# Second-layer softmax denominators by 32x32 transposes and row sums, with a moved sum written in place, narrower low products and an earlier range check

## The chip, the cores and the metric

The kernel runs on one core of a Trainium2 chip. The metric is the device time of one execution in microseconds (us). The core's engines are TensorE (PE for its matmuls, PEld for its weight loads), VectorE (DVE), ScalarE (ACT), GpSimd (POOL) and SyncE (SP, which issues DMAs). Each works through its own queue in order, and semaphores tie them together.

## The reference, cut to what matters

Two attention layers follow each other on four images of 64 x 64 tokens with 256 channels, in fp32:

```python
# layer 0: N = 4096 tokens, C = 256, q and k of 32 channels, v of 256
q, k, v = x @ Wq + bq, x @ Wk + bk, x @ Wv + bv
attn = softmax(q @ k.T)                 # per image, 4096 x 4096
x = gamma * (attn @ v) + x
# layer 1: f and g of 32 channels, v of 128, Wo from 128 to 256
f, g, v = x @ Wf + bf, x @ Wg + bg, x @ Wh + bh
beta = softmax(g @ f.T)
x = x + (beta @ v) @ Wo + bo
```

## The kernel before, in words

The kernel never subtracts a maximum: it takes exp of the raw scores, divides at the end by the sum of the exponentials, and at its very end checks that all denominators, values and gamma lay in a safe range (a general path, not taken with these inputs, stands behind that check).

**Blocks and steps.** The work is one long list of `Step`s: for each image `b`, each layer `l`, each block `j` of queries, each step `i` over the keys. The first layer has 16 blocks of 256 queries and 8 steps of 512 keys; the second has 8 blocks of 512 queries and 16 steps of 256 keys. So there are 512 steps of the first layer and 512 of the second, in 32 blocks, one execution long. Each step handles a tile of 128 x 1024 scores: `scores` (L532 the products, L542 and L544 the exponentials), products with the values (`products_first`, L580, and `products_second`, L598), and on VectorE what follows.

**Split and whole steps.** In every step of the first layer and in the steps `SPLIT1` of the second, the exponentials are cut into parts of reduced precision: `high` (L542, ACT), `low` = p - high (`cut_low`, L555, DVE) and `d` (`cut_both`, L560, DVE). Such products run as one instruction each. In the other steps the whole fp32 `p` is multiplied (two instructions for each product).

**Denominators.** In the first layer the values carry two more columns (`W` = 258 instead of `C` = 256): column 256 holds 1.0 in the high part, 0.0 in the low part and -EPS in the d part, so the denominators come out of the products themselves. The second layer's accumulator is turned the other way (128 channels x 512 queries), so there the sums over the keys are made apart: DVE adds up the `p` tiles of a block (`add_up`, L571 and L573) into `p_sum`; the tiles of the steps `MOVED_SUMS` are left to DMAs that POOL issues, the first as a copy (L548) and the others accumulating (L550), into the buffer `p_sum_moved`. `end_second` (run when a block's last step is traced) adds the accumulator's second half to the first (L655), adds `p_sum_moved` to `p_sum` (L657) and the two halves of `p_sum` to each other (L658, `sums`, 128 x 512). Each of the 128 partitions then still holds its own part of the sum, and queries lie along the row. For each of the four groups of 128 queries, `output(t)` multiplies the attention output by `Wo` (L665), multiplies `sums` with a column of ones (L666), which adds over the partitions and turns the result, takes the reciprocal (L668), scales (L671, `y`) and adds `y` to the output in DRAM by an accumulating DMA (L673).

**What sets the order.** `plan` puts units of work into the steps of a block: the four `output` units of the block before into steps 1 to 4, and the projections (L392 transpose, L422, L464 and what follows) of the next image into steps of this one. The loop at L733 calls, in each step: `cut_both`, `cut_low` of the next step, `add_up`, `scores` two steps ahead, the units, the products. The framework places all semaphores and gives out the buffers; an instruction whose buffer is not free yet is queued later than its place in the program says, and a POOL DMA may be queued earlier when its buffer is free. For example the loads of queries (L493, `q`, four DMAs) of block j + 2 stand in POOL's queue near the end of block j.

**Buffers.** `wide` gives tiles of 128 x 1024: tag "t" has two buffers (`high`, and `p` of split steps of the second layer), "p" three, "l" two (`low`, and `d` of the second layer), "d" one (`d` of the first layer, `p_sum`), "e" one (`p_sum_moved`). Small tiles of 128 x 256 (`small`) have four. The accumulators (`acc`) have one buffer each. PSUM tiles for side products (`side_psum`) have two.

**End.** After the last block the range check runs (L805 to L820), writes a count (`off`), and every engine loads that count and branches past the general path.

Of the kernel before, what the change touches and what calls it, by code (L numbers as in the profile page):

```python
# [50 lines left out]
F32 = mybir.dt.float32  # L51
# [3 lines left out]
ALU = mybir.AluOpType  # L55
AX = mybir.AxisListType

P = 128
QB = 512
QB0 = 256  # L60
NT = QB // P
S = 32
# [3 lines left out]
AHEAD = 3  # L66

SPLIT1 = (0, 3, 5, 8, 11, 13)
MOVED_SUMS = (0, 4, 7, 9, 12)

# [166 lines left out]
def fast_path(ctx: ExitStack, tc: tile.TileContext, x, w0, w1, wo, bo, gamma, out, off):  # L239

    nc = tc.nc
    B, N, C = x.shape
# [24 lines left out]
    def wide(tag, name, dtype=F32):  # L267
        return work.tile([P, 2 * QB], dtype, tag=tag, bufs={"d": 1, "e": 1, "p": 3}.get(tag, 2), name=name)
# [39 lines left out]
    ones = const.tile([P, 1], F32, name="ones")  # L308
    nc.vector.memset(ones, 1.0)

    inverse = const.tile([P, 2, B * N // P], F32, name="inverse")
    seen_v = const.tile([P, 2, B * NH], F32, name="seen_v")
    down = const.tile([P, 1], F32, name="down")
# [32 lines left out]
    def side_psum(name):  # L346
        return ps_side.tile([P, QB], F32, tag="side", name=name)
# [25 lines left out]

    xT, x_parts, k_t, v_t, halves = {}, {}, {}, {}, {}
    qk_dram, x1_dram = {}, {}
    q_t, moved_sums, first_p, waiting = {}, {}, [], {}


    def transpose_unit(b, l, h):
# [130 lines left out]
    def small(name):  # L510
        return work.tile([P, C], F32, tag="small", bufs=4, name=name)


    class Step:
# [8 lines left out]
        def scores(self):  # L523
            b, l, j, i = self.b, self.l, self.j, self.i
            n = 2 * QB // G[l]
            q0 = j * n % QB
            index = j * NI[1] + i
            tag = "pair" if l == 1 and index > 0 and index % 2 == 0 else "st"
            st = ps_main.tile([P, G[l], n], F32, tag=tag, name=f"st_{self.key}")
            for g in range(G[l]):  # L530
                kt = G[l] * i + g
                nc.tensor.matmul(  # L532
                    st[:, g, :],
                    k_t[b, l, kt // NT][:, kt % NT * P : (kt % NT + 1) * P],
                    q_t[b, l, j * n // QB][:, q0 : q0 + n],
                    start=True,
                    stop=True,
                )
            s_flat = st.rearrange("p g n -> p (g n)")
            if self.split:  # L540
                self.high = wide("t", f"high_{self.key}", F32R)
                nc.scalar.activation(self.high, s_flat, AF.Exp, bias=down)  # L542
            self.p = wide("t" if self.split and l == 1 else "p", f"p_{self.key}")
            nc.scalar.activation(self.p, s_flat, AF.Exp)  # L544
            if l == 1 and i in MOVED_SUMS:
                if i == MOVED_SUMS[0]:
                    moved_sums[b, j] = wide("e", f"p_sum_moved_{b}_{j}")
                    nc.gpsimd.dma_start(moved_sums[b, j], self.p)  # L548
                else:
                    nc.gpsimd.dma_start(moved_sums[b, j], self.p, accum_op=ALU.add)  # L550

        def cut_low(self):
            if self.split:
# [7 lines left out]
                    self.d, self.low.bitcast(F32), -UP, self.high.bitcast(F32), ALU.mult, ALU.add  # L561
                )

        def add_up(self, p_sum):
            if self.l == 0 or self.i in MOVED_SUMS:
                return
            kept = [i for i in range(NI[1]) if i not in MOVED_SUMS]
            if self.i == kept[0]:
                first_p.append(self.p)
            elif self.i == kept[1]:  # L570
                nc.vector.tensor_add(p_sum, first_p.pop(0), self.p)  # L571
            else:
                nc.vector.tensor_add(p_sum, p_sum, self.p)  # L573

        def products_first(self, acc, s, what):
            p, v, which = {
                "h": (self.high, "h", 0), "l": (self.low, "l", 0), "d": (self.d, "d", 1)
            }[what]
            for g in range(G[0]):
                nc.tensor.matmul(  # L580
                    acc[2 * s + which][:, :W],
                    p[:, g * QB0 + s * P : g * QB0 + (s + 1) * P],
                    v0[self.i][v][:, g, :],
                    start=self.first and what != "l" and g == 0,
                    stop=self.last and what != "h" and g == G[0] - 1,
                )
# [62 lines left out]
            nc.scalar.activation(o[h][:, :QB0], acc[0][:, h * QB0 : (h + 1) * QB0], AF.Copy, scale=1.0 + EPS)  # L649
        return o  # L650

    def end_second(b, j, acc, p_sum, o):
        key = f"{b}_{j}"
        for h in range(QB // QB0):
            nc.vector.tensor_add(o[h][:, :QB0], o[h][:, :QB0], acc[1][:, h * QB0 : (h + 1) * QB0])  # L655
        sums = work.tile([P, QB], F32, tag="sums", bufs=1, name=f"sums_{key}")
        nc.vector.tensor_add(p_sum, p_sum, moved_sums[b, j])  # L657
        nc.vector.tensor_add(sums, p_sum[:, :QB], p_sum[:, QB:])  # L658

        def output(t):  # L660
            def issue():
                tok = slice(t * P, (t + 1) * P)
                ps = side_psum(f"pso_{key}_{t}")
                part = o[t // NS][:, t % NS * P : (t % NS + 1) * P]
                nc.tensor.matmul(ps[:, :C], part, wo_sb, start=True, stop=True)  # L665
                nc.tensor.matmul(ps[:, C : C + 1], sums[:, tok], ones[:, :1], start=True, stop=True)  # L666
                n = (b * N + j * QB) // P + t
                nc.vector.reciprocal(inverse[:, 1, n : n + 1], ps[:, C : C + 1])  # L668

                y = small(f"y_{key}_{t}")  # L670
                nc.scalar.activation(y, ps[:, :C], AF.Copy, scale=inverse[:, 1, n : n + 1])  # L671
                row = j * QB + t * P
                nc.gpsimd.dma_start(out[b, row : row + P, :], y, accum_op=ALU.add)  # L673

            return issue

        return [output(t) for t in range(NT)]

    def run(units):
        for u in units:  # L680
            u()


    x_res = {}
# [10 lines left out]
    beyond = Step(B, 1, 0, 0)  # L695
    beyond.scores, beyond.split = nothing, False
    keys = [(b, l, j) for b in range(B) for l in range(2) for j in range(NB)][NB:]
    acc, p_sum, units = None, None, {}

    def plan(b, l, j, ends):  # L700

        units = {}

        def put(i, *some):
            units.setdefault(i, []).extend(some)

        if l == 0:

            if j >= 2:
                t, qk, v = project_units(b, 1, j - 2)  # L710
                put(0, t), put(4, qk), put(5, v)
            for n, u in enumerate(ends):
                put(1 + n, u)
            return units
        if j == 0:
            for n, u in enumerate(ends):
                put(1 + n, u)
            for n, h in enumerate((NH - 2, NH - 1)):
                t, qk, v = project_units(b, 1, h)
                put(6 * n, t), put(6 * n + 2, qk), put(6 * n + 3, v)  # L720
        else:
            for n, u in enumerate(ends):
                put(1 + n, u)
        if b + 1 < B:
            for h in range(NH):
                i = 12 + 7 * h - j * NI[1]
                for n, u in zip((0, 2, 3), project_units(b + 1, 0, h)):
                    if 0 <= i + n < NI[1]:
                        put(i + n, u)
        return units  # L730

    ends = bias_units()
    for n, s in enumerate(steps):  # L733
        b, l, j = s.b, s.l, s.j
        if s.first:
            units = plan(b, l, j, ends)
            acc = [ps_main.tile([P, QB], F32, tag=f"acc{a}", name=f"acc{a}_{b}_{l}_{j}") for a in range(2)]
            if l == 0:
                pair = ps_main.tile([P, 2, QB], F32, tag="pair", name=f"acc_pair_{b}_{j}")
                acc += [pair[:, a, :] for a in range(2)]  # L740
            if l == 1:
                p_sum = wide("d", f"p_sum_{b}_{j}")
        if l == 0 and s.last:
            x_res[b, j] = []
            for t in range(NS):
# [18 lines left out]

        s.cut_both()
        after.cut_low()
        s.add_up(p_sum)
        todo = units.get(s.i, [])

        if l == 1:  # L770
# [26 lines left out]
        while keys and halves.get(keys[0]) == 2 and (keys[0][:2] == (b, l) or keys[0][2] < over):  # L797
            load_k(*keys.pop(0))
        if s.last:
            ends = end_first(b, j, acc) if l == 0 else end_second(b, j, acc, p_sum, o)  # L800
    run(ends)

    good = small("good").rearrange("p (l n) -> p l n", l=2)  # L805
    nc.vector.tensor_scalar(good, inverse, 1.0 / SUM_MAX, None, ALU.is_ge)
    nc.vector.tensor_scalar(inverse, inverse, 1.0 / SUM_MIN, None, ALU.is_le)
    nc.vector.tensor_mul(good, good, inverse)
    nc.vector.tensor_scalar(seen_v, seen_v, VALUE_MAX, None, ALU.is_le)
    size = const.tile([P, 1], F32, name="size")  # L810
    nc.vector.tensor_mul(size, gamma_sb, gamma_sb)
    nc.vector.tensor_scalar(size, size, GAMMA_MAX**2, None, ALU.is_le)
    low = const.tile([P, 1], F32, name="low")
    for seen, axes in ((good, AX.XY), (seen_v, AX.XY)):
        nc.vector.tensor_reduce(low, seen, axes, ALU.min)
        nc.vector.tensor_mul(size, size, low)
    nc.vector.tensor_scalar(low, size, 1.0, None, ALU.is_lt)
    count = ps_side.tile([1, 1], F32, tag="side", name="count")
    nc.tensor.matmul(count, ones, low, start=True, stop=True)
# [51 lines left out]
```

## Time and profile before

| what | value |
|---|---|
| median of 3 runs | 3157.75 us (3157.27 to 3158.47) |
| the profiled execution's own time | 3156.87 us |
| its span, first to last instruction | 3155.1 us |
| granted TensorE clock, mean | 0.998 |
| a late block of the second layer (last image, nothing of a next image beside it) | 35.51 us |
| a block of the second layer with projections of the next image | 39.4 to 41.9 us |
| a block of the first layer, most | 28.2 to 28.5 us |

The profile is of one execution. Its page gives the busy time of each engine, the span in 40 slices, the DMA queues, the chain that ended last (followed back from the last instruction, at each step to what released it), the costliest groups of instructions and the DMA issues. A group line reads: line of the kernel, engine, operation, output <- inputs, partitions x elements, count | busy us in total, mean ns of one | idle time of the engine just before them and what ended it. Timelines give start us, duration us, engine, line, operation, with the idle time before it in brackets. Matmuls are pipelined: the duration of one overlaps the next, so what a matmul costs is read from one start to the next, or from the chain, whose pieces follow each other.

### The profile page before, as it was taken

What the parts mean: (1) busy time and instruction counts of PE and PEld (TensorE: products, weight loads), DVE (VectorE), ACT (ScalarE), POOL (GpSimd) and SP (SyncE); (2) the same over time, 40 slices, a digit from 0 to 9 for tenths busy, and PEclk for the clock granted to TensorE, in tenths of its full rate; (3) what the DMA queues carried; (4) which work ended last, traced back from release to release, by engine and by line L of the source; (5) the groups of instructions that cost most, each with busy time, mean ns of one, the idle gap of its engine ahead of it and who ended that gap; (6) DMA issues with size and microseconds to landing.
All of it is one profiled execution on the core that took longest, in us unless ns stands there. A gap on an engine that the chain in (4) does not pass through costs nothing.

```text
span 3155.1 us, 54090 instructions
## 1 busy us (share of the span) xinstructions
PE 3117.6 (99%) x19908; PEld 2674.3 (85%) x19908; DVE 2689.3 (85%) x3237; ACT 2138.5 (68%) x2835; POOL 898.7 (28%) x1108
## 2 busy tenths in 40 slices
PE   8999999999999999999999999999999999999997
PEld 7999998666799999866689999976668999996664
DVE  7888888888888888988888888888888888888876
ACT  7666666777666666777766666677776666666664
POOL 5222224222422222422242222332223222233221
PEclk9999999999999999999999999999999999999999
DMA  4121114555512121455541112255554111125454
GB/s 122 40 53 47 47 49 104 108 105 107 102 43 51 43 51 47 113 101 112 107 94 45 50 44 53 51 117 105 106 113 80 48 46 46 49 66 105 97 96 73
DMA packets 391392, 239.49 MB, mean 76 GB/s; under 512 B 266672, under 2 KB 355248, under 8 KB 391120
## 3 DMA queue, kind: packets, MB, share of 16 engines
q0 software_dynamic: 68160, 134.86, 22.0%
q1 hardware_dynamic: 322048, 100.76, 13.3%
q8 instruction: 161, 2.64, 0.4%
q14 instruction: 111, 0.91, 0.1%
q10 hardware_dynamic: 912, 0.33, 0.0%
HBM read 82.58 MB, written 67.11 MB: 47 GB/s over the span
## 4 chain that ended last, share of the span: by engine, by line
PE 91%; DVE 3%; issue 2%; DMA 2%; ACT 1%; POOL 0%; SPq 0%; DVEq 0%; ACTq 0%; POOLq 0%
PE acc L580 23%; PE acc_pair L580 23%; PE acc L598 23%; PE st L532 14%; PE psv L464 4%; PE psqk L422 2%; PE pso L665 2%; DVE low L555 1%; DMA squares<-in_x 1%; DVE d L560 1%; ACT p L544 1%; DVE p_sum L573 1%; DMA p_sum_moved<-p 0%; PE pso L666 0%; DMA squares<-x_dram 0%
## 5 line engine op out<-in xcount | busy, mean ns | idle before, releaser
L542 ACT ACTIVATE high<-st,down 128x1024 fp32r<-128x1024 f32 x704 | 785.8, 1116 | 707.2 <-PE st L532 419.5
L544 ACT ACTIVATE p<-st 128x1024 f32<-128x1024 f32 x1024 | 1042.2, 1021 | 167.5 <-PE st L532 145.8
L560 DVE SCALAR_TENSOR_TENSOR d<-low,high 128x1024 fp32r<-128x1024 f32 x704 | 870.5, 1237 | 227.7 <-PE acc_pair L580 222.3
L555 DVE TENSOR_TENSOR low<-p,high 128x1024 fp32r<-128x1024 f32 x704 | 938.5, 1333 | 142.7 <-ACT p L544 141.7
L532 PE MATMUL st<-q,k 128*128 128x256 f32 (+1 forms) x3072 | 703.7, 337 | 2.8 <-issue 1.3
L598 PE MATMUL acc<-p,v 128*128 128x512 f32 x1280 | 611.0, 597 | 0.0
L532 PEld LDWEIGHTS st<-q,k 128*128 128x128 f32 x3072 | 470.7, 189 | 102.9 <-issue 41.3
L637 POOL TENSOR_TENSOR x_res<-x,bo 128x256 f32<-128x256 f32 x128 | 213.9, 1671 | 879.5 <-DVE x L626 879.4
L598 PEld LDWEIGHTS acc<-p,v 128*128 128x128 f32 x1280 | 233.2, 189 | 161.8 <-issue 143.4
L573 DVE TENSOR_TENSOR p_sum<-p_sum,p 128x1024 f32<-128x1024 f32 x288 | 352.6, 1224 | 10.4 <-ACT p L544 6.8
L580 PE MATMUL acc<-v0h,high 128*128 128x258 f32 x2048 | 342.4, 284 | 1.2 <-ACT high L542 1.2
L580 PE MATMUL acc<-v0d,d 128*128 128x258 f32 x2048 | 339.3, 287 | 2.4 <-DVE d L560 2.0
L580 PE MATMUL acc<-v0l,low 128*128 128x258 f32 x2048 | 331.5, 283 | 0.6 <-DVE low L555 0.5
L580 PE MATMUL acc_pair<-v0l,low 128*128 128x258 f32 x2048 | 331.1, 283 | 0.0
L580 PE MATMUL acc_pair<-v0h,high 128*128 128x258 f32 x2048 | 329.6, 283 | 0.0
L580 PE MATMUL acc_pair<-v0d,d 128*128 128x258 f32 x2048 | 329.0, 283 | 0.0
L580 PEld LDWEIGHTS acc<-v0h,high 128*128 128x128 f32 x2048 | 287.2, 189 | 3.1 <-issue 1.4
L580 PEld LDWEIGHTS acc<-v0d,d 128*128 128x128 f32 x2048 | 280.9, 189 | 5.4 <-DVE d L560 4.7
L580 PEld LDWEIGHTS acc<-v0l,low 128*128 128x128 f32 x2048 | 281.7, 190 | 1.8 <-DVE low L555 1.3
L580 PEld LDWEIGHTS acc_pair<-v0h,high 128*128 128x128 f32 x2048 | 282.4, 189 | 0.0
L580 PEld LDWEIGHTS acc_pair<-v0l,low 128*128 128x128 f32 x2048 | 281.8, 189 | 0.0
L580 PEld LDWEIGHTS acc_pair<-v0d,d 128*128 128x128 f32 x2048 | 281.8, 189 | 0.0
(108 smaller groups left out, 3326.6 us busy)
## 6 DMA issues: line engine op xcount, KB each, us to landing
p_sum_moved<-p POOLq DMA_DIRECT2D x160, 512.0 KB, 4.8
x_res<-in_x SPq DMA_DIRECT2D x128, 128.0 KB, 2.1
qk_dram<-qk_parts SPq DMA_DIRECT2D x128, 128.0 KB, 1.8
x_dram<-x SPq DMA_DIRECT2D x128, 128.0 KB, 1.7
out<-x_res SPq DMA_DIRECT2D x128, 128.0 KB, 1.7
squares<-x_dram SPq DMA_DIRECT2D x512, 32.0 KB, 2.0
out<-y POOLq DMA_DIRECT2D x128, 128.0 KB, 3.2
q<-qk_dram POOLq DMA_DIRECT2D x252, 64.0 KB, 2.2
```

What stands on the lines that cost most here:

```text
L422: nc.tensor.matmul(ps, wqk[l][:, c, :], x_parts[key][n][:, c, :], start=(c == n == 0), stop=(c == NCC - 1 and n == 1),)
L464: nc.tensor.matmul(ps[:, t, :], xT[key][:, c, t * P : (t + 1) * P], wv[l][:, c, :], start=(c == 0), stop=(c == NCC - 1),)
L532: nc.tensor.matmul(st[:, g, :], k_t[b, l, kt // NT][:, kt % NT * P : (kt % NT + 1) * P], q_t[b, l, j * n // QB][:, q0 : q0 + n], start=Tru ...
L542: nc.scalar.activation(self.high, s_flat, AF.Exp, bias=down)
L544: nc.scalar.activation(self.p, s_flat, AF.Exp)
L555: nc.vector.tensor_sub(self.low, self.p, self.high.bitcast(F32))
L560: nc.vector.scalar_tensor_tensor(self.d, self.low.bitcast(F32), -UP, self.high.bitcast(F32), ALU.mult, ALU.add)
L573: nc.vector.tensor_add(p_sum, p_sum, self.p)
L580: nc.tensor.matmul(acc[2 * s + which][:, :W], p[:, g * QB0 + s * P : g * QB0 + (s + 1) * P], v0[self.i][v][:, g, :], start=self.first and ...
L598: nc.tensor.matmul(acc[which], v_part[:, g, :], p[:, g * QB : (g + 1) * QB], start=first and g == 0, stop=last and g == G[1] - 1,)
L637: nc.gpsimd.tensor_add(x_old[s], x_new[s], bo_sb)
L665: nc.tensor.matmul(ps[:, :C], part, wo_sb, start=True, stop=True)
```

## The change

The change touches only the fast path. It does seven things.

1. In the second layer, all blocks but the last get their denominators from a new unit pair instead of the four products with ones. `turn` transposes `sums` in 32 x 32 blocks on DVE and adds up each block's rows there (`part_sums`, 128 x 16); `denominators` multiplies that with a constant `same` (128 x 128, 1.0 where two indices agree modulo 32) and takes four reciprocals of 32 partitions x 4. They are put into steps 1 and 2 of the next block, and the four `output` units move to steps 3 to 6.
2. `sums` is written in place into the first half of `p_sum`, and the transpose goes into its second half, so `p_sum`'s buffer is held until the row sums are made. The new block's `p_sum` is taken when its second kept step is added instead of at its first step.
3. `MOVED_SUMS` has six steps, 3, 4, 7, 9, 12 and 14, instead of five (0, 4, 7, 9, 12).
4. The first of them, step 3, is written by ACT straight into the "e" buffer; no copy is issued, and the five others accumulate into it.
5. The first layer's low products use 256 columns instead of 258, except in each block's last step.
6. The range check of all denominators but those of the last block moves into step 13 of the last block; only the last 4 columns are checked at the end, in a "t" buffer instead of a small one.
7. `same` is built on POOL at the start, by a copy, three additions and three copies of 128 x 32.

```diff
-MOVED_SUMS = (0, 4, 7, 9, 12)
+MOVED_SUMS = (3, 4, 7, 9, 12, 14)
...
+    same = const.tile([P, P], F32, name="same")
+    nc.gpsimd.tensor_copy(same[:, :S], ident[:, :S])
+    for a in range(1, P // S):
+        nc.gpsimd.tensor_add(same[:, :S], same[:, :S], ident[:, a * S : (a + 1) * S])
+    for a in range(1, P // S):
+        nc.gpsimd.tensor_copy(same[:, a * S : (a + 1) * S], same[:, :S])
...
-            self.p = wide("t" if self.split and l == 1 else "p", f"p_{self.key}")
+
+            base = l == 1 and i == MOVED_SUMS[0]
+            self.p = wide("e" if base else "t" if self.split and l == 1 else "p", f"p_{self.key}")
             nc.scalar.activation(self.p, s_flat, AF.Exp)
-            if l == 1 and i in MOVED_SUMS:
-                if i == MOVED_SUMS[0]:
-                    moved_sums[b, j] = wide("e", f"p_sum_moved_{b}_{j}")
-                    nc.gpsimd.dma_start(moved_sums[b, j], self.p)
-                else:
-                    nc.gpsimd.dma_start(moved_sums[b, j], self.p, accum_op=ALU.add)
+            if base:
+                moved_sums[b, j] = self.p
+            elif l == 1 and i in MOVED_SUMS:
+                nc.gpsimd.dma_start(moved_sums[b, j], self.p, accum_op=ALU.add)
...
-        def add_up(self, p_sum):
+        def add_up(self):
             if self.l == 0 or self.i in MOVED_SUMS:
                 return
             kept = [i for i in range(NI[1]) if i not in MOVED_SUMS]
             if self.i == kept[0]:
                 first_p.append(self.p)
-            elif self.i == kept[1]:
-                nc.vector.tensor_add(p_sum, first_p.pop(0), self.p)
-            else:
-                nc.vector.tensor_add(p_sum, p_sum, self.p)
+                return
+            so_far = first_p.pop(0) if self.i == kept[1] else p_sums[self.b, self.j]
+            if self.i == kept[1]:
+                p_sums[self.b, self.j] = wide("d", f"p_sum_{self.b}_{self.j}")
+            nc.vector.tensor_add(p_sums[self.b, self.j], so_far, self.p)
...
+            width = C if what == "l" and not self.last else W
             for g in range(G[0]):
                 nc.tensor.matmul(
-                    acc[2 * s + which][:, :W],
+                    acc[2 * s + which][:, :width],
                     p[:, g * QB0 + s * P : g * QB0 + (s + 1) * P],
-                    v0[self.i][v][:, g, :],
+                    v0[self.i][v][:, g, :width],
...
-        sums = work.tile([P, QB], F32, tag="sums", bufs=1, name=f"sums_{key}")
+        p_sum = p_sums[b, j]
         nc.vector.tensor_add(p_sum, p_sum, moved_sums[b, j])
-        nc.vector.tensor_add(sums, p_sum[:, :QB], p_sum[:, QB:])
+        sums, squares = p_sum[:, :QB], p_sum[:, QB:]
+        nc.vector.tensor_add(sums, sums, squares)
+        n0 = (b * N + j * QB) // P
+        end = b == B - 1 and j == NQ[1] - 1
+        part_sums = work.tile([P, QB // S], F32, tag="part_sums", bufs=1, name=f"part_sums_{key}")
+
+        def turn():
+
+            nc.vector.transpose(squares, sums)
+            nc.vector.tensor_reduce(part_sums, squares.rearrange("p (n k) -> p n k", k=S), AX.X, ALU.add)
+
+        def denominators():
+
+            ps = side_psum(f"psd_{key}")[:, : QB // S]
+            nc.tensor.matmul(ps, same, part_sums, start=True, stop=True)
+            for a in range(P // S):
+                rows = slice(a * S, (a + 1) * S)
+                of_rows = ps[rows, :].rearrange("p (t a) -> p t a", a=P // S)[:, :, a]
+                nc.vector.reciprocal(inverse[rows, 1, n0 : n0 + NT], of_rows)
...
-                nc.tensor.matmul(ps[:, C : C + 1], sums[:, tok], ones[:, :1], start=True, stop=True)
-                n = (b * N + j * QB) // P + t
-                nc.vector.reciprocal(inverse[:, 1, n : n + 1], ps[:, C : C + 1])
+                n = n0 + t
+                if end:
+                    nc.tensor.matmul(ps[:, C : C + 1], sums[:, tok], ones[:, :1], start=True, stop=True)
+                    nc.vector.reciprocal(inverse[:, 1, n : n + 1], ps[:, C : C + 1])
...
-        return [output(t) for t in range(NT)]
+        return ([] if end else [turn, denominators]) + [output(t) for t in range(NT)]
...
+    def check(values):
+        good = wide("t", f"good_{values.shape[1]}")[:, : values.shape[1]]
+        worst = work.tile([P, 1], F32, tag="g", name=f"worst_{values.shape[1]}")
+        nc.vector.tensor_scalar(good, values, 1.0 / SUM_MAX, None, ALU.is_ge)
+        nc.vector.tensor_scalar(values, values, 1.0 / SUM_MIN, None, ALU.is_le)
+        nc.vector.tensor_mul(good, good, values)
+        nc.vector.tensor_reduce(worst, good, AX.X, ALU.min)
+        nc.vector.tensor_mul(size, size, worst)
...
+        if (b, j) == (B - 1, NQ[1] - 1):
+            put(NI[1] - 3, check_all_but_last)
...
-            if l == 1:
-                p_sum = wide("d", f"p_sum_{b}_{j}")
```

`check_all_but_last` squares and compares gamma, compares the largest values (`seen_v`), and calls `check` on all denominators but the last four columns; after the last outputs `check` is called on those four.

## The prediction

> **What bounds the kernel now.** I read the page's busy shares and its chain that ended last, then the groups of instructions by form, then the chain and the engines' timelines in one late block, and last the end of the chain. The first two say that TensorE (PE) is the bound:
>
> ```profile
> PE 3117.6 (99%) x19908; PEld 2674.3 (85%) x19908; DVE 2689.3 (85%) x3237; ACT 2138.5 (68%) x2835; POOL 898.7 (28%) x1108
> PE 91%; DVE 3%; issue 2%; DMA 2%; ACT 1%; POOL 0%; SPq 0%; DVEq 0%; ACTq 0%; POOLq 0%
> ```
>
> An instruction taken from PE is worth its full pitch; one put on DVE is free while DVE (85%) delivers in time. The groups by form give the durations:
>
> ```profile
> L573 DVE TENSOR_TENSOR p_sum<-p_sum,p 128x1024 f32<-128x1024 f32 x288 | 352.6, 1224 | 10.4 <-ACT p L544 6.8
> L580 PE MATMUL acc<-v0l,low 128*128 128x258 f32 x2048 | 331.5, 283 | 0.6 <-DVE low L555 0.5
> L392 DVE STREAM_TRANSPOSE xT<-squares 128x512 f32<-128x512 f32 x112 | 78.9, 705 | 15.3 <-DMA squares<-x_dram 6.5 <-DMA squares<-in_x 4.9 <-issue 3.4
> L666 PE MATMUL pso<-ones,sums 128*128 128x1 f32 x256 | 36.2, 211 | 0.2
> L668 DVE RECIPROCAL inverse<-pso 128x1 f32<-128x1 f32 x128 | 20.5, 162 | 15.3 <-PE pso L666 14.2
> L815 DVE TENSOR_REDUCE low<-good 128x1 f32<-128x256 f32 x1 | 0.4, 420 | 0.0
> ```
>
> A matmul's mean overlaps its neighbours, so PE is priced from the chain of waits, whose pieces do not overlap (start us, us, what). This is a block of the second layer of the last image; one such block takes 35.51 us (DVE's L655 at 2958.66 and 2994.17):
>
> ```profile
> 2995.51 0.43 PE pso L665 x2
> 2995.94 0.12 PE pso L666 x2
> 2996.06 2.30 PE acc L598 x6
> ...
> 3008.35 2.18 PE acc L598 x6
> ```
>
> A denominator product (two instructions, as all whole fp32 products here) takes 0.12 and makes the six products behind it 0.12 longer (2.30 against 2.18); the start times give 0.028 + 0.112 + 0.083 = 0.223. I use 0.225.
>
> **The change, part by part.** (1) *Ones products.* 32 blocks x 4; the last block keeps them. 124 x 0.225 = 27.9 us off PE, on the path.
>
> (2) *The product with `same`.* One for 31 blocks, weights 128x128 as before, 16 columns instead of 1. Nearest row: the ones pair, 0.225. L598 takes 0.429 per pass of 512 columns, 0.84 ns a column, so 15 more columns in two passes add at most 0.025; the far end is the L665 pair with 256 columns, 0.43. I take 0.235: 7.3 us (7.0 to 13.3).
>
> The Trainium skill, "TensorE: Matmul & The Clock Gate", section "Back-to-back issue gap", gives 1 to 64 columns about 60 cycles, 25 ns. By it (1) would be an estimated 6.2 us and (2) 1.6, and the two would gain 4.6 instead of 20.6; the 0.12 + 0.12 of the chain speaks against it here, since each of the two passes loads its own weights.
>
> (3) *256 columns for the low products.* 448 of the 512 steps of the first layer (all but each block's last) x 8 = 3584 matmuls. From start to start in groups of four, the 258-column low products take 119.7 ns, the 256-column scores of the same steps 118.2: 1.4 ns, 5.0 us. Bounds: two columns at the 0.45 ns a column of the 512-column scores (231 ns from start to start) give 3.2 us; the projections L422, also 256 columns, have 115.8 ns, which gives 14.0.
>
> (4) *VectorE.* Out goes one full-width add per block (1.22), since six steps instead of five are summed by DMA. In come a transpose of 128x512 (0.705) and a reduce of 128x512 to 16: L815 takes 0.42 for 256 elements, and 512 in place of them add at most as much again, so 0.42 to 0.84; I take 0.69, L658's time for 512 elements. Four reciprocals remain four. Net +0.17 per block, 5 us on an engine that idles 7 us in each 35.5. The Trainium skill, "VectorE: DVE Perf Modes", section "Rules for kernel authors", calls the reduce on a hot path the slowest DVE op and advises against it; no row here shows one on this path. What matters is when: the block end.
>
> ```profile
> 2989.44 2.55 DVE L573 TENSOR_TENSOR p_sum<-p_sum,p 128x1024 f32<-128x1024 f32 x2
> 2993.04 1.22 DVE L657 TENSOR_TENSOR p_sum<-p_sum,p_sum_moved 128x1024 f32<-128x1024 f32 x1
> 2994.17 0.75 DVE L655 TENSOR_TENSOR o<-o,acc 128x256 f32<-128x256 f32 x2
> 2994.84 0.69 DVE L658 TENSOR_TENSOR sums<-p_sum 128x512 f32<-128x512 f32 x1
> 2995.44 1.22 DVE L560 SCALAR_TENSOR_TENSOR d<-low,high 128x1024 fp32r<-128x1024 f32 x1
> ```
>
> DVE runs here without a gap. One of the two adds at 2989.44 goes. After d (2996.65) come the transpose and the reduce, to 2997.95 (pitch 0.65 each), then the next block's first sum, which reuses p_sum's one buffer and so can't come before the reduce. PE loses an output (0.65) from step 1 and would reach the `same` product at 2998.07. So it is just in time, and I cost it at nothing; the cover is 0.1 us. DVE then does the new first sum in the place of L571, and the low of step 3 (2998.85) stays about where it is. If an order with something else ahead of the reduce was made, PE waits (second rival). Outputs move from steps 1-4 to 3-6, and their transfers on POOL with them: nothing reads those, and four y buffers cover them.
>
> (5) *Moved sums.* Five DMAs a block stay five: the copy L548 (0.55 on POOL, landing after 2.9) becomes an accumulation like L550 (0.87, landing after 4.5 to 5.4). ACT now writes step 3 into the sum's buffer, so ACT instead of POOL waits for L657 (done 2994.3); it gets there at 2997.8, so this costs nothing, and with 3.5 us less cover the next scores would follow. The accumulation of step 4 must wait for the low of step 3 (done 3000.1); it starts at 3000.39 today. Step 14's is new, late, and stands on POOL beside these:
>
> ```profile
> 2983.31 0.86 POOL L550 DMA_DIRECT2D p_sum_moved<-p  x1 [4.21 <-DMA p_sum_moved<-p]
> 2988.21 2.01 POOL L493 DMA_DIRECT2D q<-qk_dram  x4 [4.04 <-PE st L532]
> ```
>
> It adds into the same buffer, so it waits for step 12's landing (2983.31 + 4.56 = 2987.87); with the usual 0.5 it issues at 2988.4 and lands at 2992.9. L657, which needs it, starts at 2993.04 today. I cost it at nothing, with 0.1 us to spare and 0.4 more before PE notices (L655 ends at 2994.9; PE will write that accumulator from 2995.35).
>
> (6) *Image boundaries.* Three times the next block is of the first layer, whose d uses p_sum's buffer and now waits for transpose and reduce: up to 1.35 us each on PE, 4.0 us; 0 if other work fills in.
>
> (7) *Range check.* Today it starts only when the first y has landed:
>
> ```profile
> 3138.01 3.05 DMA out<-y
> ...
> 3141.34 0.34 DVE good L806
> ```
>
> The last reciprocal ends at 3139.44, off is written at 3144.40: 4.96. The new rest is six operations on 4 columns, pitch 0.19 as L816, and the last 0.68: 1.9, so 3.0 gained. The big part (L806 to L816 again, 2.6 us) stands on DVE in step 13 ahead of the final sums, of which one add (1.3) went: 1.3 lost. Net 1.7 (0.4 to 3.0). Building `same` is seven small operations on POOL (its 128x128 ones take 0.20 and 0.32), about 2 us of the 4.06 that POOL idles before its first k load: nothing.
>
> Sum: 27.9 - 7.3 + 5.0 + 1.7 - 4.0 = 23.3. The profiled execution took 3156.87 (span 3155.1), so 3133.6; it lay 0.88 below the median of three, 3157.75, so 3134.5.
>
> **The rivals.** *The accumulation of step 14 lands late (slower).* If POOL issues the four q loads (2.01) first, it lands at 2994.9. DVE waits at L657, and behind that in its queue stand L655 and d, for which PE waits. 1.6 us in the 24 blocks that load a q at their end is 38: 3173. It decides from a lateness of 1.4 us on (23.3/24 + 0.4). For it: both wait for events of 2987.9 and the order is set when the program is built. Against it: the sum comes earlier in the program. 14%.
>
> *PE waits for the row sums.* The reduce late by 0.4 us in 31 blocks: 12.4, 3147; late by the 1.2 of one more DVE operation it would be 34 and no gain is left. For it: gapless DVE from 2986 to 2998. Against: where PE has other products ready, the order can put them first. 15%.
>
> *The two columns are worth more*, as L422's pitch says: 9 us better, 3125.5. 9%.
>
> *It does less than it says*: the last block's 4 ones products and 64 steps' low products stay; that is in the counts.
>
> **How the numbers follow.** The forecast has 62%: 3134.5, its own range 3121 (14.0 for the columns, nothing lost at the boundaries) to 3144 (13.3 for `same`, 3.2 for the columns, 0.4 for the check). The range reaches on through the second rival to 3156 and leaves out the first rival. What a measurement can tell from no change is about 0.2%, 6.3 us: 3151.4 to 3164.1. Faster: forecast 0.62, columns 0.09, two thirds of the second rival 0.10, together 0.81. Same 0.05. Slower 0.14.
>
> **What would show it.** Right: 8 ones matmuls and 62 with `same`; a late block of 34.9 us; the low products' pitch near 118; L657 starting without a wait for a DMA; off written within 2.5 us of the last reciprocal. Wrong: idle PE before `same` (DVE reduce) or before the products of step 1 behind L655; a DVE wait on p_sum_moved's landing; a late block not under 35.5.

## The result, and the profile after

| | before | after |
|---|---|---|
| median | 3158.11 us (3157.27 to 3160.84, 4 runs) | 3212.81 us (3208.42 to 3215.57, 4 runs) |
| ratio, 95% interval | | 1.017 (1.0157 to 1.0182) |
| profiled execution, its span | 3156.87, 3155.1 us | 3208.42, 3206.6 us |
| granted TensorE clock, mean (1.00 in the late block shown below) | 0.998 | 0.993 |
| late block of the second layer (median of blocks 2 to 6 of the last image) | 35.51 us | 37.67 us |

The changed kernel is 1.7% slower, 54.7 us; the forecast was 3134.5, faster by 0.74%. From here on, a block's length runs from ScalarE's first `p` of it to the first `p` of the next. The page after, busy shares and the chain that ended last by engine and by line:

```profile
PE 3123.3 (97%) x19722; PEld 2659.5 (83%) x19722; DVE 2701.6 (84%) x3272; ACT 2141.5 (67%) x2835; POOL 905.7 (28%) x1115
PE 82%; DMA 7%; DVE 5%; issue 3%; ACT 1%; POOL 1%; SPq 0%; DVEq 0%; POOLq 0%; ACTq 0%
```

PE has 186 instructions fewer, as planned, but its share of the chain fell from 91% to 82%, and DMA rose from 2% to 7%. The waits of the changed kernel name the transfer (engine, line, waited for: us in total, times, longest):

```profile
DVE p_sum L667 <- DMA p<-p: 46.5, 27, 3.8
...
PEld acc L608 <- DVE low L562: 21.3, 24, 1.7
PE acc L608 <- DVE o L665: 18.4, 18, 2.5
...
PEld acc L608 <- DVE o L665: 12.3, 9, 1.5
...
PE acc L608 <- DVE low L562: 11.4, 18, 1.3
```

L667 adds the moved sum to `p_sum` (L657 before). It waits in 27 of 32 blocks, unevenly: 13 of these waits are longer than 2 us and hold 36.5 of the 46.5 us. PE waits for two things that do not use the moved sum: `low` (L562) and the adds of `o` (L665). One late block shows why. VectorE's timeline:

```profile
3030.23 1.22 DVE L581 TENSOR_TENSOR p_sum<-p_sum,p 128x1024 f32<-128x1024 f32 x1
3034.23 1.23 DVE L667 TENSOR_TENSOR p_sum<-p_sum,p 128x1024 f32<-128x1024 f32 x1 [2.78 <-DMA p<-p]
3035.37 1.22 DVE L562 TENSOR_TENSOR low<-p,high 128x1024 fp32r<-128x1024 f32 x1
3036.51 0.68 DVE L669 TENSOR_TENSOR p_sum<-p_sum 128x512 f32<-128x512 f32 x1
3037.11 1.22 DVE L567 SCALAR_TENSOR_TENSOR d<-low,high 128x1024 fp32r<-128x1024 f32 x1
3038.36 0.75 DVE L665 TENSOR_TENSOR o<-o,acc 128x256 f32<-128x256 f32 x2
3039.02 0.70 DVE L676 STREAM_TRANSPOSE p_sum<-p_sum 128x512 f32<-128x512 f32 x1
3039.76 0.69 DVE L677 TENSOR_REDUCE part_sums<-p_sum 128x16 f32<-128x512 f32 x1
```

POOL's timeline in the same block:

```profile
3023.84 0.88 POOL L557 DMA_DIRECT2D p<-p  x1 [4.86 <-ACT p L553]
3028.93 0.87 POOL L557 DMA_DIRECT2D p<-p  x1 [4.21 <-DMA p<-p]
3029.47 2.35 POOL L500 DMA_DIRECT2D q<-qk_dram  x4
```

And PE's:

```profile
3036.64 0.73 PE L608 MATMUL acc<-low,v 128*128 128x512 f32 x2 [1.26 <-DVE low L562]
...
3039.16 1.98 PE L608 MATMUL acc<-p,v 128*128 128x512 f32 x4 [1.10 <-DVE o L665]
```

Step 14's accumulation (128 x 1024, 512 KB) is issued at 3028.93 and lands 5.21 later, at 3034.1; VectorE stands at L667 from 3031.45 on. The `p` that `low` needs was done at 3032.2 (ACT's timeline), so `low` comes 3.1 us late and `o` after it. Before, the order was `low`, L657, `o`, last adds, `d`; now it is L667, `low`, last adds, `d`, `o`. In `e1` (below), which gives VectorE that one add back, the order is the old one again, and L667 waits for nothing. That the framework sets the order from its own estimate of when each input will be there, and has the DMA land earlier than it does, is inferred from these orders and not shown. The Trainium skill, "TensorE: Matmul & The Clock Gate", section "Architectural detail: the array is 16× 32×32, not 1× 128×128", says that the vector engine takes its queue strictly in order; the trace agrees: `low` stood ready behind the waiting L667 for 2 us.

A stop of PE may cost more than its own length. Between 200 us and the end of the last block, the granted TensorE clock is 1.00 throughout in the kernel before. In the changed kernel it is 0.5 in eight stretches of 3.4 us, each of which begins inside or within 2 us behind a stop of PE of 1.5 to 2.5 us. Here is one of them: first the stretch with the stop, then the one at half clock (window, its length, then busy us and count of PE, PEld, DVE, ACT and POOL, granted clock, DMA share, GB/s), then the four products that run into it, 3.10 us where four such took 1.98 above:

```profile
728.00:733.00 5.00, 1.87 (x7) 1.08 (x7) 5.00 (x9) 2.02 (x3) 0.00 (x0) 1.00 0.16 39
733.00:736.40 3.40, 3.40 (x7) 1.67 (x6) 3.30 (x4) 1.23 (x2) 0.00 (x0) 0.51 0.00 0
...
732.38 3.10 PE L608 MATMUL acc<-p,v 128*128 128x512 f32 x4 [2.50 <-DVE o L665]
```

With PE busy all through them, eight such stretches are worth an estimated 8 x 3.41 / 2 = 13.7 of the 54.7 us. The late block above has none.

### The profile page after: what moved, and what is told of

Same layout as the page of the kernel before. It is cut to its first block, busy times and chain, and to the rows that moved or that the text cites. A ratio compares the mean times of both kernels' runs of the same rounds, so it can differ in the third digit from the quotient of the medians.

```text
span 3206.6 us, 53841 instructions
## 1 busy us (share of the span) xinstructions
PE 3123.3 (97%) x19722; PEld 2659.5 (83%) x19722; DVE 2701.6 (84%) x3272; ACT 2141.5 (67%) x2835; POOL 905.7 (28%) x1115
## 4 chain that ended last, share of the span: by engine, by line
PE 82%; DMA 7%; DVE 5%; issue 3%; ACT 1%; POOL 1%; SPq 0%; DVEq 0%; POOLq 0%; ACTq 0%
PE acc L590 22%; PE acc_pair L590 22%; PE acc L608 17%; PE st L539 12%; DMA p<-p 6%; PE psv L471 4%; PE pso L693 2%; PE psqk L429 2%; DVE low L562 1%; DVE d L567 1%; ACT p L553 1%; DMA squares<-x_dram 1%; POOL k L500 0%; DVE o L665 0%; DMA squares<-in_x 0%
## 5 line engine op out<-in xcount | busy, mean ns | idle before, releaser
L562 DVE TENSOR_TENSOR low<-p,high 128x1024 fp32r<-128x1024 f32 x704 | 935.2, 1328 | 123.9 <-ACT p L553 123.2
L647 POOL TENSOR_TENSOR x_res<-x,bo 128x256 f32<-128x256 f32 x128 | 203.9, 1605 | 846.9 <-DVE x L636 846.7
L557 POOL DMA_DIRECT2D p<-p x160 | 142.1, 888 | 758.7 <-ACT p L553 308.2
L590 PE MATMUL acc<-v0l,low 128*128 128x256 f32 (+1 forms) x2048 | 329.7, 283 | 7.0 <-DVE low L562 6.9
L590 PE MATMUL acc_pair<-v0l,low 128*128 128x256 f32 (+1 forms) x2048 | 329.5, 282 | 0.0
L581 DVE TENSOR_TENSOR p_sum<-p_sum,p 128x1024 f32<-128x1024 f32 x256 | 311.9, 1218 | 15.2 <-ACT p L553 13.9
```

The lines of the kernel that those rows point to most:

```text
L562: nc.vector.tensor_sub(self.low, self.p, self.high.bitcast(F32))
L581: nc.vector.tensor_add(p_sums[self.b, self.j], so_far, self.p)
L590: nc.tensor.matmul(acc[2 * s + which][:, :width], p[:, g * QB0 + s * P : g * QB0 + (s + 1) * P], v0[self.i][v][:, g, :width], start=self.f ...
L647: nc.gpsimd.tensor_add(x_old[s], x_new[s], bo_sb)
```

## The experiments

Medians; each ratio is to runs of the kernel before on the same chip (3158.4 to 3160.0). The other columns are of the one profiled execution. Late: a late block, as above. First: mean of the blocks j = 0 of the first three images. Behind: the first-layer block behind an image's end. Half clock: us at a granted clock of 0.5 between 200 us and the end of the last block; PE loses up to half of it.

| kernel | us | ratio, 95% interval | late | first | behind | half clock |
|---|---|---|---|---|---|---|
| before | 3158.1 | | 35.51 | 37.1 | 29.1 | 0 |
| after | 3212.8 | 1.017 (1.0157 to 1.0182) | 37.67 | 40.4 | 31.6 | 27.3 |
| e1_five | 3170.3 | 1.0039 (1.0025 to 1.0053) | 35.26 | 40.6 | 29.7 | 10.2 |
| e2_order | 3177.1 | 1.0064 (1.0047 to 1.0081) | 35.17 | 40.1 | 30.6 | 6.8 |
| e3_before_six | 3215.8 | 1.0177 (1.0158 to 1.0196) | 38.1 to 42.1 | 37.1 | 31.8 | 37.5 |
| e4_cols | 3155.5 | 0.9991 (0.9982 to 1.0) | 35.51 | 37.2 | 29.1 | 0 |
| e5_moved_as_before | 3159.6 | 1.0002 (0.9993 to 1.0012) | 35.43 | 37.6 | 29.7 | 0 |
| e6_same_later | 3149.6 | 0.997 (0.9958 to 0.9982) | 35.30 | 37.2 | 29.3 | 0 |
| e7_copy3 | 3168.3 | 1.0027 (1.0015 to 1.0039) | 35.51 | 39.8 | 29.6 | 13.7 |
| e8_total_in_e | 3145.1 | 0.9957 (0.9942 to 0.9972) | 35.31 | 37.2 | 27.7 | 0 |
| e9_order_later | 3169.7 | 1.0032 (1.0018 to 1.0047) | 34.83 | 40.0 | 30.7 | 13.7 |
| e10_all_four | 3148.4 | 0.9966 (0.9954 to 0.9979) | 34.83 | 37.4 | 29.2 | 0 |
| e11_before_six_order | 3161.2 | 1.0005 (0.9994 to 1.0015) | 35.6 | 37.5 | 29.6 | 0 |
| e12_last_five | 3141.2 | 0.9943 (0.9929 to 0.9957) | 34.83 | 38.7 | 27.7 | 3.4 |

**Step 14, and its place in the queue.** Three kernels take apart which step is moved and where its sum is added. `keep_in_program_order` keeps an instruction behind all that was traced before it on its engine.

```diff
 # e1_five, from after
-MOVED_SUMS = (3, 4, 7, 9, 12, 14)
+MOVED_SUMS = (3, 4, 7, 9, 12)
 # e2_order, from after
-        nc.vector.tensor_add(p_sum, p_sum, moved_sums[b, j])
+        tc.keep_in_program_order(nc.vector.tensor_add(p_sum, p_sum, moved_sums[b, j]))
 # e3_before_six, from before
-MOVED_SUMS = (0, 4, 7, 9, 12)
+MOVED_SUMS = (0, 4, 7, 9, 12, 14)
```

> The changed kernel with five moved steps (3, 4, 7, 9, 12): step 14 is added by VectorE again, everything else stays. Late sum (step 14's accumulation lands too late, VectorE waits for it at the add of the moved sum, and behind that stand low, d and the adds of o): the loss goes, about 3137 us (3130 to 3145), a late block of 34.9 us, no wait of L667 for a DMA. Rival, row sums (the transpose, the reduce and the held p_sum buffer cost the time): 3190 or more. Rival, base in place (step 3 written into the sum's buffer makes ScalarE and step 4's accumulation wait): 3190 or more.

> The changed kernel with the add of the moved sum (L667) kept behind everything traced before it on VectorE: low, d of the next block's step 0 and both adds of o now stand ahead of it. All six moved steps stay. Late sum, with the order as the cause: PE no longer waits although the DMA lands as late as before; about 3140 us (3133 to 3155), a late block of 34.9 to 35.3. Late sum, with the landing itself as the cause (the row sums then come too late for the product with same): 3195 or more, with PE idle ahead of L682. Row sums or base in place: 3200 or more.

> The kernel before with step 14 as a sixth moved step (0, 4, 7, 9, 12, 14) and nothing else of the change. Late sum: slower by 1.5 to 2.8 us in each of 32 blocks, 3200 to 3245 us, with L657 ahead of low in VectorE's queue and waiting for the DMA by some 2.8 us. Row sums or base in place: one add less on VectorE and no loss, 3150 to 3160.

`e3` settles that moving step 14 is enough for harm of this size: 3215.8 us without any other part of the change. `e1` and `e2` get most of it back, 42.5 and 35.7 us, but both end more than 20 us above their expected ranges: something else is lost as well. `e2` keeps step 14's DMA and changes only the order. Its late block on VectorE:

```profile
3009.54 1.23 DVE L562 TENSOR_TENSOR low<-p,high 128x1024 fp32r<-128x1024 f32 x1 [0.82 <-ACT p L553]
3010.87 1.23 DVE L567 SCALAR_TENSOR_TENSOR d<-low,high 128x1024 fp32r<-128x1024 f32 x1
3012.12 0.75 DVE L665 TENSOR_TENSOR o<-o,acc 128x256 f32<-128x256 f32 x2
3012.79 1.22 DVE L667 TENSOR_TENSOR p_sum<-p_sum,p 128x1024 f32<-128x1024 f32 x1
```

The accumulation was issued at 3006.18 and landed 5.20 later, at 3011.4, as late as in the changed kernel; L667, now behind `d` and `o`, comes at 3012.79 and waits for nothing; it does not wait for a DMA in any of the 32 blocks. `e11` repeats this on the kernel before:

```diff
 # e11_before_six_order, from e3_before_six
-        nc.vector.tensor_add(p_sum, p_sum, moved_sums[b, j])
+        tc.keep_in_program_order(nc.vector.tensor_add(p_sum, p_sum, moved_sums[b, j]))
```

> As e3_before_six (the kernel before with step 14 moved too, 3215.8 us), with the add of the moved sum (L657) kept behind everything traced before it on VectorE. Queue order as the cause of e3's loss: most of it goes, 3155 to 3175 us; step 0's copy now waits for the later add, which may keep some. The landing itself as the cause: 3200 or more.

From 3215.8 to 3161.2 by the place of one instruction. It is no gain over the kernel before, though: on its own, the sixth moved step brings nothing. In `e3` VectorE waits 4.63 us at L657 and the adds of `o` end at 3047.4; in `e11` `o` goes first, and nothing waits. A late block of each, VectorE, `e3` first:

```profile
3042.68 1.23 DVE L657 TENSOR_TENSOR p_sum<-p_sum,p_sum_moved 128x1024 f32<-128x1024 f32 x1 [4.63 <-DMA p_sum_moved<-p]
...
3046.69 0.75 DVE L655 TENSOR_TENSOR o<-o,acc 128x256 f32<-128x256 f32 x2
```

```profile
2999.35 0.75 DVE L655 TENSOR_TENSOR o<-o,acc 128x256 f32<-128x256 f32 x2
3000.01 1.22 DVE L657 TENSOR_TENSOR p_sum<-p_sum,p_sum_moved 128x1024 f32<-128x1024 f32 x1
```

**What else was lost.** `e5` undoes the moved sums altogether and keeps the rest.

```diff
 # e5_moved_as_before, from after
-MOVED_SUMS = (3, 4, 7, 9, 12, 14)
+MOVED_SUMS = (0, 4, 7, 9, 12)
...
             if base:
-                moved_sums[b, j] = self.p
+                moved_sums[b, j] = wide("e", f"p_sum_moved_{b}_{j}")
+                nc.gpsimd.dma_start(moved_sums[b, j], self.p)
```

(In it, `p` of that step goes to its former buffer.)

> The changed kernel with the moved sums as in the kernel before: steps 0, 4, 7, 9, 12, the first one copied by a DMA. Late sum: as with the five steps, within 6 us of e1_five, about 3137 us (3130 to 3145). Base in place: about 3137 too, but then e1_five is at 3190 or more. Row sums: 3190 or more.

3159.6: 11 us better than `e1`, but no gain over the kernel before and 15 above the expected range. Two losses show in `e5` and `e1`. The first, in both, is ahead of the product with `same`. The chain of waits in a late block of `e5`, then of `e9` (start us, us, what):

```profile
3000.97 0.47 PE st L539 x2
3001.44 0.02 issue
3001.47 0.39 PE psd L683 x2
3001.86 1.81 PE acc L609 x4
```

```profile
3016.38 0.13 PE psd L682 x2
3016.51 1.01 PE acc L608 x4
```

In `e5` the product stands 0.39 in the chain, not 0.13: by start times, the scores ahead of it take 0.419 instead of 0.234, and its first half 0.132 instead of 0.027. It waits for the reduce. `e6` gives it one step more, `e9` does the same for `e2` (`nothing` is an empty unit):

```diff
 # e6_same_later, from e5; e9_order_later, from e2
-        return ([] if end else [turn, denominators]) + [output(t) for t in range(NT)]
+        return ([] if end else [turn, nothing, denominators]) + [output(t) for t in range(NT)]
```

> As e5_moved_as_before (the changed kernel with the moved sums of before), but with the product with same put one step later, into step 3, and the outputs into steps 4 to 7. In e5 the instruction ahead of same stands 0.19 us too long and same's first half 0.10 too long in a late block, 35.43 us against the 34.84 that the prediction's terms give. Row sums just too late: that goes, a late block of 34.85 to 35.15 us and about 3150 us (3144 to 3154). If what is left of the gain was lost elsewhere: 3157 to 3162 as e5.

> As e2_order (all six moved steps, the add of the moved sum kept behind the adds of o), with the product with same in step 3 as in e6. In a late block of e2 the scores ahead of same stand 0.21 us too long and same's first half 0.10: 0.31 us in 31 blocks, 9.6 us. Row sums just too late: 3167 us (3162 to 3172), a late block of 34.85, the 34.84 of the prediction's terms, since one add less stands on VectorE than in e6 (35.30). If another wait takes its place: 3174 to 3180.

`e6` gains 10.0 us and `e9` 7.4 by the medians; by the ratios both gain some 10. In `e6` a late block stays at 35.30, since `low` of step 5 now comes 0.4 us late for PE: ScalarE's `high` of that step waits 2.0 us for an add of VectorE to `p_sum`; in `e9`, with step 14's add off VectorE, it is 34.83.

The second loss, the larger one in `e1`, is in the first block of each image's second layer, 40.6 us in `e1`, 37.6 in `e5` and 37.1 before. `e7` tells the choice of step from the writing in place:

```diff
 # e7_copy3, from e5
-MOVED_SUMS = (0, 4, 7, 9, 12)
+MOVED_SUMS = (3, 4, 7, 9, 12)
```

> As e1_five (steps 3, 4, 7, 9, 12 moved), but with step 3 copied into the sum's buffer by a DMA instead of written there. The first block of an image's second layer (j = 0) took 41.2 us in e1, 37.2 with the steps 0, 4, 7, 9, 12 of e5. If the cause is that step 0 is summed by VectorE again and its adds stand ahead of the new x that the next projections wait for: j = 0 stays at 41 us, the total at about 3168 us (3164 to 3172). If the writing in place is the cause: 37.2 us and about 3159 (3155 to 3162).

39.8 us and 3168.3 in all: it is the choice, not the writing in place (`e1`, 3170.3; the intervals of the two overlap). Step 0 goes back to VectorE, and its sums stand ahead of the new x that the next projections need. VectorE in the first block of the first image, `e7`, then `e5` (L637 writes x, L399 transposes what was loaded back of it):

```profile
525.16 1.22 DVE L582 TENSOR_TENSOR p_sum<-p,p 128x1024 f32<-128x1024 f32 x1
526.48 1.23 DVE L582 TENSOR_TENSOR p_sum<-p_sum,p 128x1024 f32<-128x1024 f32 x1
529.19 0.87 DVE L637 SCALAR_TENSOR_TENSOR x<-o,g,x_res 128x256 f32<-128x256 f32 x2
...
541.17 0.70 DVE L399 STREAM_TRANSPOSE xT<-squares 128x512 f32<-128x512 f32 x1
```

```profile
524.35 0.48 DVE L637 SCALAR_TENSOR_TENSOR x<-o,g,x_res 128x256 f32<-128x256 f32 x1
...
525.98 0.96 DVE L637 SCALAR_TENSOR_TENSOR x<-o,g,x_res 128x256 f32<-128x256 f32 x1
...
537.03 0.70 DVE L399 STREAM_TRANSPOSE xT<-squares 128x512 f32<-128x512 f32 x1
```

The block begins at 521.28 in `e7` and at 519.99 in `e5`. Counted from there, x is ready 1.8 us later (8.8 against 7.0) and the transpose starts 2.8 later (19.9 against 17.0). The waits of `e7` end at PE, where the same line has 0.9 us in `e5`:

```profile
PE st L539 <- DMA k<-qk_dram: 9.5, 4, 2.8
```

All four first blocks of `e7` have such a wait of 2.0 to 2.8 us near their end, and the clock is at 0.5 for 3.4 us behind each; `e5` has no such stretch.

**Columns and the image's end.** `e4` is the kernel before with the narrower low products alone; `e8` frees `p_sum`'s buffer early at the end of an image:

```diff
 # e8_total_in_e, from e6
-        nc.vector.tensor_add(p_sum, p_sum, moved_sums[b, j])
-        sums, squares = p_sum[:, :QB], p_sum[:, QB:]
+        total = moved_sums[b, j] if j == NQ[1] - 1 else p_sum
+        nc.vector.tensor_add(total, p_sum, moved_sums[b, j])
+        sums, squares = total[:, :QB], total[:, QB:]
```

> The kernel before with the low products of 256 columns alone. The forecast's price is 1.4 ns for each of 3584 products, 5.0 us: 3153.4 us by the median of 3158.4 in this series. The first layer's blocks of the changed kernel, 28.21 us against 28.25, say 0.6 ns, 2.3 us: about 3156 (3154.5 to 3157.5).

> As e6_same_later, but in the last block of each image the add of the moved sum writes into the moved sum's buffer, so that p_sum's buffer, which the first layer's d uses, comes free without waiting for transpose and reduce. In e5 the two first-layer blocks behind each image's end are longer by 0.5 and 0.8 us than in the kernel before. If the held buffer is the cause (the forecast's 4.0 us for three boundaries): 3 to 4 us below e6, about 3146 us. If not: as e6.

The columns are worth about 2.8 us by the ratio, 0 to 5.7 by its interval (3.9 by the medians). From start to start in groups of four, the median over the run, the low products take 118.7 ns instead of 119.3. The held buffer cost 4.5 us at three image ends.

**All together.** `e10` keeps the whole change with these four points mended, `e12` leaves step 14 on VectorE in an image's last block, where the next block waits for the buffer:

```diff
 # e10_all_four, from e9
+MOVED_FIRST = (1, 4, 7, 9, 12, 14)
+def moved(j):
+    return MOVED_FIRST if j == 0 else MOVED_SUMS
...
+        total = moved_sums[b, j] if j == NQ[1] - 1 else p_sum
 # e12_last_five, from e10
-    return MOVED_FIRST if j == 0 else MOVED_SUMS
+    return MOVED_FIRST if j == 0 else MOVED_SUMS[:5] if j == 7 else MOVED_SUMS
...
+        if j < NQ[1] - 1:
+            tc.keep_in_program_order(add)
```

> The changed kernel with all four causes mended and all six moved steps kept: the add of the moved sum behind the adds of o, same in step 3, the total of an image's last block in the moved sum's buffer, and in the first block of an image the steps 1, 4, 7, 9, 12, 14 moved in place of 3, 4, 7, 9, 12, 14, so that the first sum on VectorE comes as late there as before. From e9: 3.7 us off each of four first blocks, some 1.3 off each block behind them, 1.5 to 2 off each of three image ends: about 3142 us (3134 to 3150). If the step chosen is not what delays the first blocks: 3155 to 3165.

> As e10_all_four, but the last block of each image moves only five steps (3, 4, 7, 9, 12) and its add of the moved sum is placed freely, as in e8. The first-layer block behind an image's end took 27.69 us in e8, 29.22 in e10 and 29.12 in the kernel before. If step 14's late landing is what holds p_sum's buffer there: 1.5 us off each of three image ends, about 3144 us (3141 to 3147). If not: as e10, 3147 to 3150.

`e10` ends at 3148.4, within what was expected, and `e12` at 3141.2, the lower end of its expected range, 0.57% faster than the kernel before (0.43 to 0.71%) and the lowest median here. Its interval overlaps that of `e8` (0.28 to 0.58%), which keeps the five moved sums of the kernel before: a late block is shorter by 0.48 us in `e12`, but it is not shown that moving step 14, or step 3 in place of step 0, gains anything over the whole kernel. Its five executions lie from 3140.3 to 3148.1; the profiled one is the 3148.1, with one first block of 41.7 us against 37.2 and 37.3 in two others. The trace shows what that block lost: VectorE stood idle for 2.84 us ahead of a transpose (L405), to 0.3 us behind the landing of a load of `squares` that took 4.22 us where the seven ahead of it took 1.8 to 3.8. PE stopped for 1.58 and 0.67 us, and the clock was at 0.5 for the next 3.4 us. Why this load was late only there is open.

## Why the prediction was wrong

**Moved sums, the step that failed.** It put step 14's issue 5.1 us behind step 12's, and that is what the trace has (3023.84, 3028.93). The landing it took as 4.56 after that, by the rows of before; with the four q loads right behind it measured 5.21. But this 0.65 us is not the loss: in `e2` the DMA lands as late and nobody waits. (`e2` has L667 farther back than the kernel before; its old place, right behind `low`, was not run with this landing. In the late block above it would have waited an estimated 0.7 us there, from the end of a `low` begun at 3032.24 to 3034.13.) What failed is that the step set the landing against the place that L657 had before, behind `low`. The add that part (4) took off VectorE was what had held L657 there. With it gone the order was made anew, and a wait that no product needs came to stand ahead of three instructions that PE needs. Price by `e2`: 35.7 us, of which an estimated 10 is the clock (27.3 us at half clock against 6.8).

**Rival 1** named the right accumulation, the right wait and one of the two victims behind it (`o`; where it has `d`, the trace has `low`), and 3173. Its condition was wrong: POOL issues step 14 first, not the q loads, and a lateness of 1.4 us was not needed. The changed kernel's last block but one loads no q, its DMA lands after 4.55, and from adds of `o` to adds of `o` it still takes 37.51 us (3113.70 to 3151.21). L667 waits in 27 blocks, not 24, and not alike: block 3 of the first image took 39.47 us against 39.95 before, block 5 took 46.07 against 41.91, with a half-clock stretch in it. In a late block PE loses 1.26 + 1.10 and some 0.5 in the products around these gaps (37.67 against the 34.83 of `e9`), not 1.6. The half-clock stretches behind longer stops were in no term.

**VectorE "just in time".** The cover of 0.1 us was not there: `same` waits about 0.3 us in a late block, rival 2's case (0.4 us, 12.4 us). Price by `e6` and `e9`: 10.0 and 7.4 us by the medians. In the changed kernel itself the wait is hidden, because PE is already late.

**Choice of steps.** The prediction followed ScalarE's wait for the buffer that step 3 is written into, and did not ask what step 0, now summed on VectorE, stands ahead of. In a late block nothing; in an image's first block, the new x. Price: `e7` against `e5`, 8.8 us by the medians, 7.9 by the ratios.

**What held.** The ones products and `same` were priced at 0.225 and 0.235, net 0.665 a block. Where nothing waits, in `e9`, `e10` and `e12`, a late block went from 35.51 to 34.83: 0.68. The Trainium skill's 25 ns for so small a product ("TensorE: Matmul & The Clock Gate", "Back-to-back issue gap") would have given an estimated 0.15 there, so for fp32 products of two instructions the measurement decides against it. The reduce took 0.674 (median of 31) against the 0.69 assumed, the transpose 0.702. Image boundaries: 4.0 forecast, 4.5 by `e8`. Columns: 5.0 forecast, 2.8 by `e4`, under its lower bound of 3.2 but with an interval that holds both. Range check: from the last reciprocal to `off` 2.00 us (3193.22 to 3195.22) against 4.96 before, forecast 1.9. Little of it reaches the end: `e10` takes 24.6 us from the start of the last exponential to the span's end, the kernel before 25.1. The last y now lands after `off` (3197.0 against 3195.2), where before it landed ahead of it; that the end waits for it was not tested.

**The sum.** Measured 78.3 us above the forecast. In steps, each a difference of medians: order of L667 35.7 (`e2`), `same` 7.4 (`e9`), first blocks and image ends 21.3 (`e10`) and 7.2 (`e12`): 71.6. The steps come from series on different chips, and by the ratios single ones differ by up to 3 us. To the 6.7 that stay come the 4.0 that the forecast had taken off for the image ends and that `e12` no longer pays. Of these 10.7 about 2 are the columns and 1 the range check. The rest is open; PE's remaining waits for `o` (3.6 us in `e12`) and the slower first-layer blocks of the last section are in it.

## What to carry to other kernels

Taking an instruction off an in-order engine can make the scheduler put something else in the hole, and if that something waits for a transfer, everything behind it waits too: read the new order, not the old one with a gap. An add that nobody needs soon belongs behind the instructions that the bounding engine needs, pinned there if the scheduler places it otherwise. When work moves from one engine to another, ask for each kind of block what it now stands ahead of; a steady block does not show what an image's first block loses. And look at the granted clock behind each stop of the bounding engine: the stop may not be all that it costs.

## What was not expected of the hardware

- In the last image's late blocks, an accumulation of 512 KB within the core's memory lands some 4.55 us after its issue, and 5.05 to 5.21 (`after`, `e2`) with four q loads of 64 KB issued right behind it; those then take 3.9 to 5.0 us instead of 2.0 to 2.5. They slow each other although they do not touch the same data. The Trainium skill, "DMA: Bandwidth & Descriptors", section "Issuing engines are not separate DMA queues", says that transfers interleave on the same 16 engines, whichever engine issued them; these rows agree, though POOL issued both here.
- Long stops of PE and a halved granted clock go together. In all runs here, between 200 us and the end of the last block, all 17 stops of PE of 2.0 us or more (up to 3.1) had a stretch at 0.5 begin inside them or within 2 us behind; of the shorter ones down to 1.0 us some had one and most had none. Each stretch lasted 3.41 us, a few twice that. That the stop brings the lower clock on is read from this order alone; no run tested it.
- A first-layer block in the middle of an image takes 28.25 us before. With the narrower products it takes 28.21 nearly throughout in some kernels (after, `e1`, `e8`) and mostly 28.32 in others (`e5`, `e9`, `e10`), or changes between the two within one run (`e4`, `e6`, `e12`), though the kernels differ there in nothing that was meant to. In one such block (image 1, block 6, counted from 0), `e8` against `e10`, the 0.11 us are spread over 236 products, some 0.4 ns each on average. Over some 60 blocks this would be an estimated 6 us, more than the columns bring. The cause is open.
